# A state space mixer: the product by C on GpSimd, u B left in PSUM

## The chip, the cores and the metric

The program runs on one core of a Trainium2 chip. The time is device microseconds of one execution: 15,565.36 us, median of 3 runs (15,554.7 to 15,567.39). The core has five engines with a queue each, in which instructions start in order: TensorE (PE; matrix products, which land in PSUM), VectorE (DVE), ScalarE (ACT), GpSimd (POOL) and SyncE (SP, which issues transfers). The rows of weight loads, which TensorE overlaps with products, are PEld. SBUF is the large on-chip memory. PSUM has eight banks of 512 float32 columns on each of 128 partitions.

## The reference, cut to what matters

64 images of 121 tokens with 128 channels go through four pairs of layers, each added to its input: a mixer, and then a feed-forward layer (experts, two recurrent ones, a spectral one). All is float32. The change lies in the mixer, which runs four times:

```python
xz = x @ in_proj_w.T
xc, z = jnp.split(xz, 2, axis=-1)
xc = silu(conv(xc, conv_w) + conv_b)              # three taps
t = xc.transpose(0, 2, 1)
xs = jnp.stack([t, t], axis=1)                    # K = 2 directions
x_dbl = jnp.einsum('bkdl,kcd->bkcl', xs, x_proj_w)
dts, Bs, Cs = ...                                 # 8, 16 and 16 rows
delta = softplus(einsum('bkrl,kdr->bkdl', dts, dt_proj_w) + dt_proj_b)
A = -jnp.exp(A_logs)
dA = jnp.exp(delta[..., None] * A[None, :, :, None, :])
dBu = delta[..., None] * Bs * xs[..., None]
_, h = associative_scan(combine, (dA, dBu), axis=3)   # h[l] = dA[l] h[l-1] + dBu[l]
y = jnp.einsum('bkdln,bknl->bkdl', h, Cs) + Ds * xs
y = y[:, 0] + jnp.flip(y[:, 1], axis=-1)
out = layer_norm(y) * gelu(z) @ out_proj_w.T
```

The 121 tokens are the channels d of the recurrence, and it runs along l, the 256 inner channels. There are 16 states n.

## The kernel before

The activations X stay in SBUF during the whole program, tokens on the partitions. A mixer (`conv_layer`, L90) goes through the images in chunks of eight (c0, L121); eight chunks in each of four mixers make 32. A chunk begins with its layer norm, transposes, the convolution into t and the gate into g (L123 to L145; the one GpSimd instruction of a chunk, the memset of L126, zeroes the borders of xnT). Then come the scans, in two groups of four images (g0) and two directions (k): four blocks a chunk, 128 in all. At the end, in four rounds of two images, stand the layer norm over tokens, the gate, the output projection and the addition to X (L217 to L241).

A block begins with its preparation (L155 to L184). TensorE makes pb (the rows of B and C) and pd (the input of delta), each in two halves of 512 columns. S takes pb as three bf16 addends in 96 rows, made by casts of ScalarE (L164, L170, L171) and subtractions of VectorE (L165, L172). ScalarE and VectorE turn pd into delta = softplus(pd + b), by Abs and Relu (L168, L169), Exp (L175), two VectorE steps (L176, L177), Ln (L178) and two more steps (L179, L182), and u = delta t (L184). All are tiles of 121 partitions by 1024 columns, four images of 256.

The inner loop (L195) then runs over the 16 states, 2048 times in the whole program:

- L200: TensorE spreads row n of B over the partitions into pB, and row n of C into pC, by a selecting matrix sel; two matrix products of 512 columns each.
- L203: ScalarE writes exp(A delta) into one of three tiles dA, whose first column of each image stays zero.
- L208: VectorE writes u pB into hs; L209 scans hs in place, with dA; L212 multiplies hs by pC in place.
- L213 calls `add_to_y`, whose L192 adds hs to the sum py, by a matrix product with the identity, in two halves of 512 columns. For the second direction it reads hs backwards. A float32 product of 512 columns shows as two rows in the profile, so a state has four rows of L192.

The buffers: hs has three; S, u and delta have two. PSUM's eight banks are split between the pool ps_bc (two buffers of two banks, tag "bc": one goes to pB and one to pC), ps_y (py, two banks) and ps (two buffers of one bank, tag "mm", for all else: pb, pd, the convolution, the transposes, the rounds at the end).

The Tile framework puts each engine's instructions into an order when the program is built, and sets semaphores for the dependencies of tiles. Instructions that stand apart in the source, such as the preparation of a block and the states of the one before, can so stand mixed in an engine's queue. In the program before, TensorE's queue in the loop reads: py of state n-1, pC of n, pB of n+1, py of n, and so on.

Of the kernel before, what the change touches and what calls it, by code (L numbers as in the profile page):

```python
# [8 lines left out]
F32 = mybir.dt.float32  # L9
BF16 = mybir.dt.bfloat16  # L10
AF = mybir.ActivationFunctionType
ALU = mybir.AluOpType
AX = mybir.AxisListType
PSUM = bass.MemoryType.PSUM
DRAM = bass.MemoryType.DRAM

D = 121  # tokens of an image: the SSM's channels
C = 128  # model channels
L = 256  # inner channels: the SSM's sequence
NS = 16  # SSM states  # L20
E = 64  # experts
NF = 35  # STU filters: 16 phi, 16 alternating phi, 3 taps of the autoregression
FG = 7  # filters at a time
BANDS = ((0, 15), (15, 30), (30, 60), (60, 121))  # tokens that 4, 3, 2, 1 scales reach


class Ctx:
    """What all parts of the program share."""
# [12 lines left out]
def bcast(ap, n):  # L41
    """[P, G] -> [P, G, n]"""
    return ap.unsqueeze(2).to_broadcast([ap.shape[0], ap.shape[1], n])


def layer_norm(cx, pool, dst, src, eps):
    """Over the channels of each token: dst, src are [D, G, C]."""
    nc = cx.nc
    G = src.shape[1]
    mean = pool.tile([D, G], F32, name="ln_mean")  # L50
    nc.vector.reduce_sum(mean, src, axis=AX.X)
    nc.vector.tensor_scalar_mul(mean, mean, 1.0 / C)
    nc.vector.tensor_sub(dst, src, bcast(mean, C))
    sq = pool.tile([D, G, C], F32, name="ln_sq", bufs=1)
    nc.scalar.activation(sq, dst, AF.Square)
    rstd = pool.tile([D, G], F32, name="ln_rstd")
    nc.vector.reduce_sum(rstd, sq, axis=AX.X)
    nc.scalar.activation(rstd, rstd, AF.Sqrt, bias=eps[:D], scale=1.0 / C)
    nc.vector.reciprocal(rstd, rstd)
    nc.vector.tensor_mul(dst, dst, bcast(rstd, C))  # L60


def conv_weights(cx, l, wp):
    """Starts the loads of a mixer's weights."""
    nc, a, w = cx.nc, cx.a, {}

    def load(name, shape, src):
        w[name] = wp.tile(shape, F32, name=name)
        nc.sync.dma_start(w[name], src)

    p = f"L{l}_conv_"
    load("in_x", [128, 2, C], a[p + "in_x"].rearrange("(q p) c -> p q c", p=128))
    load("conv_wT", [128, 3, 2, L], a[p + "conv_wT"].rearrange("j (q p) o -> p j q o", p=128))
    load("in_zT", [C, L], a[p + "in_zT"])
    load("conv_b", [1, L], a[p + "conv_b"])
    load("x_dt", [8, 2, D], a[p + "x_dt"])
    load("dt_wT", [8, 2, D], a[p + "dt_wT"])
    load("dt_b", [D, 2], a[p + "dt_b"])
    load("A", [D, 2 * NS], a[p + "A_logs"])
    load("Ds", [D, 2], a[p + "Ds"])  # L80
    load("norm", [D, 2], a[p + "norm"])
    load("out_wT", [128, 2, C], a[p + "out_wT"].rearrange("(q p) c -> p q c", p=128))
    # B's and C's projections, three times over: for the three addends of their split.
    w["x_bc"] = wp.tile([D, 2, 3, 2 * NS], F32, name="x_bc")
    for i in range(3):
        nc.sync.dma_start(w["x_bc"][:, :, i, :], a[p + "x_bc"])
    return w


def conv_layer(cx, wts, pools, dA, sel, mean_w, ones_row):  # L90
    """x + SSM mixer(LN(x)). dA: tiles whose first column of each image is zero, which starts
    an image's recurrence afresh in a scan that runs over several images."""
    nc, X, NB = cx.nc, cx.X, cx.NB
    fixed, work, ps_bc, ps_y, ps = pools
    ident = cx.ident
    CB = min(8, NB)  # images of a chunk
    GB = 4  # images of a scan
    in_x, conv_wT, in_zT, conv_b, out_wT = (wts[x] for x in ("in_x", "conv_wT", "in_zT", "conv_b", "out_wT"))
    x_dt, dt_wT, dt_b, x_bc, A, Ds, norm = (wts[x] for x in ("x_dt", "dt_wT", "dt_b", "x_bc", "A", "Ds", "norm"))

    # in_proj and the convolution are both linear, with no bias between them: one [C, L] weight per tap.
# [6 lines left out]
    # So are dt's two projections.  # L108
# [12 lines left out]
    for c0 in range(0, NB, CB):  # L121
# [10 lines left out]
        t = work.tile([D, CB, L], F32, name="t")  # L132
# [15 lines left out]
        ysb = work.tile([D, CB, L], F32, name="ysb")  # L148
        for g0 in range(0, CB, GB):
            tg = t[:, g0 : g0 + GB, :].rearrange("p b l -> p (b l)")  # L150
            py = ps_y.tile([D, GB, L], F32, name="py")
            for k in range(2):
                # B and C of 512 columns at a time: a float32 is the sum of three bf16, exactly,
                # which one matmul by ones adds up again on all the partitions.
                S = work.tile([96, GB * L], BF16, name="S")  # L155
                rest = work.tile([96, GB * L], F32, name="rest", bufs=1)
                relu = work.tile([D, GB * L], F32, name="sp_relu", bufs=1)
                e = work.tile([D, GB * L], F32, name="sp_e", bufs=1)
                w = work.tile([D, GB * L], F32, name="sp_w", bufs=1)
# [13 lines left out]
                # softplus(v) = max(v, 0) + log1p(e), e = exp(-|v|);  # L173
                # log1p(e) = ln(w) - ((w - 1) - e) with w = fl(1 + e).
# [8 lines left out]
                u = work.tile([D, GB * L], F32, name="u")  # L183
                nc.vector.tensor_mul(u, df, tg)  # L184

                def add_to_y(src, w, start, stop):
                    """The second scan's share is flipped along the sequence."""
                    for h in range(0, GB, 2):
                        rhs = src[:, h : h + 2, :]
                        if k == 1:  # L190
                            rhs = rhs[:, :, ::-1]
                        nc.tensor.matmul(py[:, h : h + 2, :], w, rhs, start=start, stop=stop)  # L192

                add_to_y(t[:, g0 : g0 + GB, :], diag[:, k, :], k == 0, False)
                for n in range(NS):  # L195
                    pB = ps_bc.tile([D, GB * L], F32, name="pB", tag="bc")
                    pC = ps_bc.tile([D, GB * L], F32, name="pC", tag="bc")
                    for dst, row in ((pB, n), (pC, NS + n)):
                        for h in range(0, GB * L, 512):
                            nc.tensor.matmul(dst[:, h : h + 512], sel[:, row, :], S[:, h : h + 512], start=True, stop=True)  # L200
                    dAn = dA[turn % len(dA)]
                    turn += 1
                    nc.scalar.activation(  # L203
                        dAn[:, :, 1:], delta[:, :, 1:], AF.Exp, scale=A[:, k * NS + n : k * NS + n + 1]
                    )
                    hs = work.tile([D, GB, L], F32, name="hs", bufs=3)
                    hf = hs.rearrange("p b l -> p (b l)")
                    nc.vector.tensor_mul(hf, u, pB)  # L208
                    nc.vector.tensor_tensor_scan(  # L209
                        hf, dAn.rearrange("p b l -> p (b l)"), hf, 0.0, ALU.mult, ALU.add  # L210
                    )
                    nc.vector.tensor_mul(hf, hf, pC)  # L212
                    add_to_y(hs, ident[:D, :D], False, k == 1 and n == NS - 1)  # L213
            nc.scalar.copy(ysb[:, g0 : g0 + GB, :], py)

# [28 lines left out]
def conv_part(cx, l, wts):  # L244
    tc, nc = cx.tc, cx.nc
    with ExitStack() as ctx:
        enter = ctx.enter_context
        fixed = enter(tc.tile_pool(name=f"cf{l}", bufs=1))
        work = enter(tc.tile_pool(name=f"ck{l}", bufs=2))
        ps_bc = enter(tc.tile_pool(name=f"cpb{l}", bufs=2, space=PSUM))  # L250
        ps_y = enter(tc.tile_pool(name=f"cpy{l}", bufs=1, space=PSUM))
        ps = enter(tc.tile_pool(name=f"cp{l}", bufs=2, space=PSUM))
        # sel[:, r, :] picks row r of B, C: it has ones in rows r, 32 + r, 64 + r.
# [15 lines left out]
def moe_layer(cx, l):  # L269
    """x + experts(LN(x)): an expert takes a weighted sum of its 8 likeliest tokens and gives its  # L270
    result back to them, by the same weights. P has those weights, and zeros for other tokens."""
# [3 lines left out]
    EG = 4  # experts of a load  # L275
# [105 lines left out]
def rnn_layer(cx, l):  # L381
    """x + RNN over the tokens of BN(LN(x) W^T): channels on partitions, tokens by images beside."""
# [3 lines left out]
    with ExitStack() as ctx:  # L386
# [31 lines left out]
        # wx * s + (beta - mean * s), s = gamma / sqrt(var + eps)  # L418
# [8 lines left out]
        TS = 512 // NB if NB > 8 else 8  # steps of a PSUM bank  # L427
# [24 lines left out]
def stu_layer(cx, l):  # L452
    """x + the STU of LN(x) at four scales, by their weights. A scale sees, and gives, a prefix of
    the tokens, and the convolutions are causal: all scales share them, and a token's output matrices
    are the weighted sums of those of the scales that reach it."""
# [4 lines left out]
    with ExitStack() as ctx:  # L460
# [6 lines left out]
        # filters[s, f, t]: what token s gives to token t  # L467
# [3 lines left out]
        # Row s is phi, after D - 1 zeros, from place D - 1 - s on. The rows of a load step forward  # L471
        # in memory, so they come by descending s, and a matmul turns them round.
# [13 lines left out]
        # (-1)^(t - s)  # L486
# [8 lines left out]
        # the scales' weights: y_hard - y_soft + y_soft, on all partitions  # L495
# [15 lines left out]
        # the first of equal maxima alone: seen = 1 once one was  # L511
# [10 lines left out]
        # M[:, z]: band z's matrices, of scales 0 .. 3 - z  # L522
# [57 lines left out]
def metaformer_kernel(ctx: ExitStack, tc: tile.TileContext, a: dict, out: bass.AP):  # L580
    nc = tc.nc
# [3 lines left out]
    # The activations stay on the chip: tokens on partitions, images by channels beside.  # L585
# [19 lines left out]
def laid_out(inputs):  # L605
    """The inputs as the program reads them: slices, transposes and zero padding alone."""
# [55 lines left out]
```

## Time and profile before

| | |
|---|---|
| median of 3 runs | 15,565.36 us |
| span of the profiled execution | 15,534.4 us |
| mean granted clock of TensorE | 0.812 |
| L209, scan on VectorE | 2048 x 2289 ns |
| L208 and L212, products on VectorE | 2048 x 1212 and 1217 ns |
| L203, exponential on ScalarE | 2048 x 1145 ns |
| L192, sum into py on TensorE | 5444.3 us busy |
| L200, pB and pC on TensorE | 1373.8 and 1383.7 us busy |

The profile's span runs from the first to the last instruction of one execution. In the lines of groups the fields are: line, engine, operation, output from inputs, shapes, count | busy time in us, mean ns of one | idle time in us of the engine just before these instructions, and what ended most of it. In lines of the timeline they are: start and duration in us, engine, line, operation, count, and in brackets the idle time before with what ended it. In a line of stretches, the fields after the length are the busy times (with counts) of PE, PEld, VectorE, ScalarE and GpSimd, the granted clock as a share of full speed, and two fields on transfers.

The page shows the span in 40 equal slices, each digit the busy share of a slice in tenths:

```profile
PE   6777776766777777776777777777677777777799
...
DVE  8888888884888888887688888888488888888522
ACT  3333333322333333332333333323333333333222
POOL 0000000000000000000000000000000000000000
PEclk8888788876788888887788888888688888888899
```

The four mixers are the long stretches with VectorE at 8; the dips at slices 10, 19 and 20, and 29 and the last three slices are the feed-forward layers. A chunk takes 425 us.

### The profile page before, as it was taken

Reading aid. Unit: us, or ns where it says so; the run is one execution under the profiler, and the core shown is the slowest. Engines: PE = TensorE matmul, PEld = TensorE weight load, DVE = VectorE, ACT = ScalarE, POOL = GpSimd, SP = SyncE. Lnnn points to the kernel's source line nnn. Section 1 sums busy time; section 2 is a strip of 40 time slices with the busy share of each in tenths; the row PEclk is TensorE's granted clock in tenths of the full one; section 3 lists DMA queues with packets and bytes.
Section 4 is the critical chain, followed back from the end, with each engine's and each line's share of the span. In section 5 each row is a group of like instructions: output and inputs, shape, how many; then the busy total and the mean of one; then the engine's idle time right before and its main releaser. Section 6 shows DMA issues by size and latency. Waiting matters only on the chain.

```text
span 15534.4 us, 76849 instructions
## 1 busy us (share of the span) xinstructions
PE 11231.5 (72%) x28744; PEld 5111.1 (33%) x28744; DVE 11896.6 (77%) x9160; ACT 4972.8 (32%) x5572; POOL 4.3 (0%) x38
## 2 busy tenths in 40 slices
PE   6777776766777777776777777777677777777799
PEld 2322332225233323333332322322323232322466
DVE  8888888884888888887688888888488888888522
ACT  3333333322333333332333333323333333333222
POOL 0000000000000000000000000000000000000000
PEclk8888788876788888887788888888688888888899
DMA  0000000002000000000000000000000000000100
GB/s 16 0 0 0 0 0 0 1 18 84 0 0 0 0 0 0 0 1 1 3 0 0 0 0 0 0 0 1 1 0 0 0 0 0 0 0 0 28 4 6
DMA packets 84526, 66.42 MB, mean 4 GB/s; under 512 B 10547, under 2 KB 70839, under 8 KB 84151
## 3 DMA queue, kind: packets, MB, share of 16 engines
q1 hardware_dynamic: 82871, 59.41, 1.3%
q8 instruction: 225, 3.69, 0.1%
q10 hardware_dynamic: 1280, 2.10, 0.0%
q14 instruction: 150, 1.23, 0.0%
HBM read 55.43 MB, written 6.06 MB: 4 GB/s over the span
## 4 chain that ended last, share of the span: by engine, by line
DVE 53%; PE 37%; ACT 5%; issue 4%; SPq 0%; DVEq 0%; DMA 0%; ACTq 0%
DVE hs L209 20%; PE py L192 16%; DVE hs L212 14%; DVE hs L208 11%; PE acc L558 3%; PE pu L548 3%; PE pc L138 3%; PE pC L200 2%; DVE ystd L228 1%; PE pc L139 1%; PE pst L440 1%; PE po L239 1%; PE pb L163 1%; DVE sp_w L179 1%; DVE S L172 1%
## 5 line engine op out<-in xcount | busy, mean ns | idle before, releaser
L192 PE MATMUL py<-hs,ident 121*121 121x512 f32 x8192 | 5444.3, 800 | 2349.9 <-DVE hs L212 2343.1
L209 DVE TENSOR_TENSOR_SCAN hs<-dA,hs 121x1024 f32<-121x1024 f32 x2048 | 4687.9, 2289 | 136.1 <-DVE hs L208 5.5
L203 ACT ACTIVATE dA<-delta,A 121x1020 f32<-121x1020 f32 x2048 | 2338.3, 1145 | 6374.4 <-DVE hs L209 6372.4
L192 PEld LDWEIGHTS py<-hs,ident 121*121 121x121 f32 x8192 | 1711.6, 230 | 4884.1 <-DVE hs L212 3379.0
L212 DVE TENSOR_TENSOR hs<-hs,pC 121x1024 f32<-121x1024 f32 x2048 | 2492.2, 1217 | 428.6 <-PE pC L200 338.0
L208 DVE TENSOR_TENSOR hs<-u,pB 121x1024 f32<-121x1024 f32 x2048 | 2482.9, 1212 | 73.0 <-PE pB L200 69.2
L200 PEld LDWEIGHTS <-sel 96*121 96x121 bf16 x8192 | 1271.8, 155 | 2852.4 <-issue 2584.3
L200 PE MATMUL pC<-S,sel 96*121 96x512 bf16 x4096 | 1383.7, 421 | 498.5 <-DVE hs L208 498.5
L200 PE MATMUL pB<-S,sel 96*121 96x512 bf16 x4096 | 1373.8, 420 | 261.5 <-DVE hs L208 189.7
L165 DVE TENSOR_TENSOR rest<-pb,S 96x512 f32<-96x512 f32 x256 | 173.5, 678 | 701.7 <-ACT S L164 701.7
L552 DVE COPY U<-pu 128x363 f32<-128x363 f32 x320 | 171.3, 536 | 652.0 <-PE pu L548 651.4
L228 DVE RECIPROCAL ystd<-ystd 121x512 f32<-121x512 f32 x128 | 427.5, 3340 | 199.0 <-ACT ystd L227 199.0
L548 PE MATMUL pu<-filt,u 121*128 121x484 f32 (+1 forms) x1280 | 469.5, 524 | 11.5 <-DVE U L552 7.5
L558 PE MATMUL acc<-U,M 128*128 128x120 f32 (+2 forms) x2240 | 477.6, 372 | 0.4
L138 PE MATMUL pc<-w_conv,xnT 128*121 128x256 f32 x1536 | 430.2, 419 | 2.2 <-ACT xnT L131 2.2
L163 PE MATMUL pb<-t,x_bc 121*96 121x512 f32 x512 | 342.1, 756 | 120.5 <-DVE rest L165 74.3
L234 PE MATMUL pyt<-ident,ysb 121*128 121x121 f32 x512 | 115.8, 369 | 414.2 <-DVE ysb L231 414.0
L554 ACT COPY U<-pu 128x484 f32<-128x484 f32 x320 | 180.5, 564 | 677.9 <-PE pu L548 675.8
L558 PEld LDWEIGHTS acc<-U,M 128*128 128x128 f32 x2240 | 334.8, 190 | 135.7 <-issue 115.0
L167 PE MATMUL pd<-t,w_dt 121*121 121x512 f32 x512 | 296.1, 662 | 44.6 <-DVE rest L165 44.6
L138 PEld LDWEIGHTS pc<-w_conv,xnT 128*121 128x121 f32 x1536 | 280.4, 196 | 126.9 <-issue 77.0
L225 PE MATMUL pv<-ysq,mean_w 121*121 121x512 f32 x256 | 195.4, 857 | 173.9 <-ACT ysq L223 173.9
(176 smaller groups left out, 7475.3 us busy)
## 6 DMA issues: line engine op xcount, KB each, us to landing
w1g<-in_L_ffn_weight_dram SPq DMA_DIRECT2D x16, 1024.0 KB
w2g<-in_L_ffn_weight_dram SPq DMA_DIRECT2D x64, 256.0 KB
X<-in_x_dram SPq DMA_DIRECT2D x8, 484.0 KB
out_dram<-X SPq DMA_DIRECT2D x8, 484.0 KB
conv_wT<-in_L_conv_conv_wT_dram SPq DMA_DIRECT2D x4, 768.0 KB
O<-og ACTq DMA_DIRECT2D x16, 128.0 KB
oe<-O SPq DMA_DIRECT2D x4, 512.0 KB
ahead<-in_L_ffn_phi_dram SPq DMA_DIRECT2D x1, 915.1 KB
```

Of the source, the lines that this page charges most:

```text
L138: nc.tensor.matmul(pc[:, i, :], xnT[:, b + i, j : j + D], w_conv[:, j, :], start=(j == 0), stop=False)
L163: nc.tensor.matmul(pb, x_bc[:, k].rearrange("p i n -> p (i n)"), tg[:, cols], start=True, stop=True)
L167: nc.tensor.matmul(pd, w_dt[:, k, :], tg[:, cols], start=True, stop=True)
L192: nc.tensor.matmul(py[:, h : h + 2, :], w, rhs, start=start, stop=stop)
L200: nc.tensor.matmul(dst[:, h : h + 512], sel[:, row, :], S[:, h : h + 512], start=True, stop=True)
L203: nc.scalar.activation(dAn[:, :, 1:], delta[:, :, 1:], AF.Exp, scale=A[:, k * NS + n : k * NS + n + 1])
L208: nc.vector.tensor_mul(hf, u, pB)
L209: nc.vector.tensor_tensor_scan(hf, dAn.rearrange("p b l -> p (b l)"), hf, 0.0, ALU.mult, ALU.add)
L212: nc.vector.tensor_mul(hf, hf, pC)
L228: nc.vector.reciprocal(std, std)
L548: nc.tensor.matmul(pu[:, : fb - fa, :], u[:, b, :], filt[:, f0 + fa : f0 + fb, :], start=True, stop=True)
L558: nc.tensor.matmul(acc[z], M[:, z, f0 + f, :], U[:, f, :, t0:t1], start=(f0 + f == 0), stop=(f0 + f == NF - 1),)
```

## The change

In the inner loop four things change. pB keeps both buffers of the tag "bc". pC becomes two tiles of 512 columns from the pool ps (tag "mm"), and ScalarE copies each into a new SBUF tile Cs, of which there are two buffers. L208's product is written back to pB in place of hs, and the scan reads it there and writes hs. The product by C reads Cs instead of pC and is issued on GpSimd. The names of the lines after are L202 and L205 (pB, pC), L206 (the copies), L209 (the exponential), L214 (the product u B), L215 (the scan) and L218 (the product by C); lines behind the loop move down by six. The sums into py stay as they are.

```diff
                 for n in range(NS):
                     pB = ps_bc.tile([D, GB * L], F32, name="pB", tag="bc")
-                    pC = ps_bc.tile([D, GB * L], F32, name="pC", tag="bc")
-                    for dst, row in ((pB, n), (pC, NS + n)):
-                        for h in range(0, GB * L, 512):
-                            nc.tensor.matmul(dst[:, h : h + 512], sel[:, row, :], S[:, h : h + 512], start=True, stop=True)
+                    Cs = work.tile([D, GB * L], F32, name="Cs")
+                    for h in range(0, GB * L, 512):
+                        nc.tensor.matmul(pB[:, h : h + 512], sel[:, n, :], S[:, h : h + 512], start=True, stop=True)
+                    for h in range(0, GB * L, 512):
+                        pC = ps.tile([D, 512], F32, name="pC", tag="mm")
+                        nc.tensor.matmul(pC, sel[:, NS + n, :], S[:, h : h + 512], start=True, stop=True)
+                        nc.scalar.copy(Cs[:, h : h + 512], pC)
                     dAn = dA[turn % len(dA)]
                     turn += 1
                     nc.scalar.activation(
                         dAn[:, :, 1:], delta[:, :, 1:], AF.Exp, scale=A[:, k * NS + n : k * NS + n + 1]
                     )
                     hs = work.tile([D, GB, L], F32, name="hs", bufs=3)
                     hf = hs.rearrange("p b l -> p (b l)")
-                    nc.vector.tensor_mul(hf, u, pB)
+                    nc.vector.tensor_mul(pB, u, pB)
                     nc.vector.tensor_tensor_scan(
-                        hf, dAn.rearrange("p b l -> p (b l)"), hf, 0.0, ALU.mult, ALU.add
+                        hf, dAn.rearrange("p b l -> p (b l)"), pB, 0.0, ALU.mult, ALU.add
                     )
-                    nc.vector.tensor_mul(hf, hf, pC)
+                    nc.gpsimd.tensor_mul(hf, hf, Cs)
                     add_to_y(hs, ident[:D, :D], False, k == 1 and n == NS - 1)
```

## The prediction

> **What bounds the kernel now.** I read the page's busy shares, then the costliest groups, then one stretch of the timeline inside a mixer, then who waits for whom.
>
> ```profile
> PE 11231.5 (72%) x28744; PEld 5111.1 (33%) x28744; DVE 11896.6 (77%) x9160; ACT 4972.8 (32%) x5572; POOL 4.3 (0%) x38
> ...
> L209 DVE TENSOR_TENSOR_SCAN hs<-dA,hs 121x1024 f32<-121x1024 f32 x2048 | 4687.9, 2289 | 136.1 <-DVE hs L208 5.5
> ...
> L212 DVE TENSOR_TENSOR hs<-hs,pC 121x1024 f32<-121x1024 f32 x2048 | 2492.2, 1217 | 428.6 <-PE pC L200 338.0
> L208 DVE TENSOR_TENSOR hs<-u,pB 121x1024 f32<-121x1024 f32 x2048 | 2482.9, 1212 | 73.0 <-PE pB L200 69.2
> ```
>
> VectorE does 9,663 us of its 11,897 in these three groups, 4.72 us for each of the 2048 states. Idle time before them is small (637.7 us in all): inside the loop VectorE is the bound, and nothing makes it wait for long. ScalarE is a third busy, GpSimd idle. So the change takes a quarter off the bound; what decides is whether VectorE can stay fed afterwards.
>
> ```profile
> 2260.28 3.64 PE L192 MATMUL py<-hs,ident 121*121 121x512 f32 x4 [0.72 <-DVE hs L212]
> ...
> 2264.19 0.59 PE L200 MATMUL pB<-S,sel 96*121 96x512 bf16 x2
> 2264.39 1.22 DVE L212 TENSOR_TENSOR hs<-hs,pC 121x1024 f32<-121x1024 f32 x1 [0.64 <-PE pC L200]
> 2265.53 1.21 DVE L208 TENSOR_TENSOR hs<-u,pB 121x1024 f32<-121x1024 f32 x1
> 2265.66 1.98 PE L192 MATMUL py<-hs,ident 121*121 121x512 f32 x4 [0.88 <-DVE hs L212]
> 2266.84 2.29 DVE L209 TENSOR_TENSOR_SCAN hs<-dA,hs 121x1024 f32<-121x1024 f32 x1
> 2267.48 0.60 PE L200 MATMUL pC<-S,sel 96*121 96x512 bf16 x2
> 2267.92 0.59 PE L200 MATMUL pB<-S,sel 96*121 96x512 bf16 x2
> ```
>
> The sum into py waits for a finished product (0.05 us after L212 ends), then come the next pC and pB, all under the following L208 and L209: 3.2 us of TensorE work beside 3.5 us of VectorE. The same four py rows take 1.98 us or 3.64 us; the granted clock, 0.81 on average, alternates between full and half, so 38% of the time is at half.
>
> I count by chunk (eight images). GpSimd's 32 memsets of L126 mark chunks, 425.3 us apart (482.50, 907.78, 1332.46).
>
> ```profile
> 2185.75:2611.06 425.31, 302.90 (x713) 127.63 (x712) 352.81 (x252) 140.56 (x147) 0.12 (x1) 0.82 0.00 0
> ```
>
> That is VectorE busy for 352.8 us of 425.3 (third pair of numbers). A chunk holds 4 blocks (two groups, two directions) of 16 states.
>
> **Removed.** 64 products a chunk of 1.217 us leave VectorE: -77.9 us.
>
> **Products in place, in PSUM.** L208 now writes pB, and the scan reads pB. No row of VectorE writes PSUM. A PSUM input costs nothing visible (L212 with pC 1217 ns, L182 from SBUF alone 1210 ns). I take zero; bounded by those 7 ns either way for both instructions, +-30 us in the program.
>
> **Copies of C.** 4096 copies of 121x512 on ScalarE; the row of that kind is L554, 128x484 from PSUM in 0.564 us, so 0.59 us each, 2,420 us. ScalarE goes from 4,973 to 7,390 us, covered by VectorE in the loop: a state costs ScalarE 1.15 + 1.18 us against 3.51 us on VectorE. Where that cover is missing, they count below.
>
> **The product on GpSimd.** Its rows:
>
> ```profile
> L126 POOL MEMSET xnT<- 128x16 f32 x32 | 3.7, 116 | 13720.1 <-PE pz L144 10389.9 <-PE px L447 2113.8 <-PE px L376 1216.4
> masks.py:199 POOL TENSOR_SCALAR_AFFINE_SELECT ident<-ident 128x128 f32<-128x128 f32 x1 | 0.3, 292 | 0.0
> masks.py:197 POOL MEMSET ident<- 128x128 f32 x1 | 0.2, 204 | 0.3 <-POOLq L652 0.3
> ```
>
> Lower bound: the memsets' slope, (204-116)/112 = 0.79 ns a column, 0.9 us for 1024 columns with its start, but it reads nothing. Upper: the select reads one operand, 292 ns for 128 columns, 2.34 us for 1024; with a second operand at the same price 4.67. I take 2.34: the select is nearest in kind, its start would not repeat eight times, and the second operand costs something. The Trainium skill ("GPSIMD Engine Reference", section Performance versus the Vector engine) has a measured 4497 ns for a float32 add of two operands at 2048 columns; half, an estimate of 2.25 us, would take 60 us off my sum.
>
> **What the product's new place makes late.** In the built program's queues the loop runs in groups of three states a, b, c. VectorE: product a, product b, scan a, scan b, product c, scan c, then product d. TensorE: ... py a, py b, first half of pB d, **py c, second half of pB d**, pC d. pB has both "bc" buffers now, yet product d still stands behind py c, py c behind GpSimd's product c, and that behind scan c, VectorE's last work. So VectorE stops once in three states for: GpSimd 2.34 + py 1.98 + half a pB 0.30 + three handovers of 0.05 = 4.77 us at full clock; 2.34 + 3.64 + 0.53 + 0.15 = 6.66 us at half. With 38% at half that is 5.5; the idle TensorE may lose some clock, so 5.6. VectorE's own work for three states is 3 x 3.51 = 10.5 us, so a group takes 16.1 us, 5.4 a state, against 4.7 to 5 now. A block has five groups and one more state, so five such stops; 20 a chunk: 112 us, where today's loop idles 637.7/32 = 19.9. **+92 us.**
>
> **Between blocks.** L165 to L184 now stand in one run on VectorE, with no state between, so their handovers are bare. The second L165 waits for pb and the cast S (1.10 + 0.58 + handovers: 1.9); L172 for two casts of 1.04 (2.2); L176 for L168, L169, L175 (0.69 + 0.68 + 1.05, less 1.22 of L172: 1.3); L179 for Ln, queued on ScalarE behind four copies of C (4 x 0.59 + a table load 1.28 + 1.06, less L176 and L177: 3.3). Sum 8.7 a block. Today: L172, L179 and L176 idle 103.1 + 66.0 + 36.8 us over 128 blocks, 1.6 a block, and L165 some 0.6 outside the chunk starts (701.7 us, of which about 19.6 at each of 32 starts, unchanged by the edit). 4 x (8.7 - 2.2) = **+26 us.**
>
> **The chunk's end.** The four rounds L221 to L241 likewise stand in a row; today some lie between states. Each waits for Sqrt (longest today 3.5 us) and for po (longest 3.9): 4 x 7.4 = 29.6, where L228 and L241 idle (199.0 + 248.1)/32 = 14.0 today. **+16 us.**
>
> **Sum.** -77.9 + 92 + 26 + 16 = +56 us a chunk, times 32 = +1,790 us on the span of 15,534.4: 17,325. The median of the runs lies 31 us above that span, so **17,350 us**. What the program does outside the mixers isn't touched.
>
> **A rule on the shared port.** No row of before has VectorE and GpSimd side by side. The Trainium skill ("SBUF — State Buffer", section Who interferes with whom) says that a VectorE instruction with two SBUF inputs excludes a GpSimd one that reads SBUF, and that one with a single SBUF input doesn't. By it the loop is free, since product and scan each take one input from pB, and only the runs between blocks could collide. No run here shows it yet.
>
> **Rivals.**
> 1. *GpSimd becomes the bound.* From about 2.9 us a product, the three products no longer fit beside scan b, product c and scan c (5.8 us). A group is then 4.72 us (products a, b and scan a) + three GpSimd products + 3.2 us (py, half a pB, handovers): 18.4 at 3.5 us, hence +2.3 x 640 stops = +1,470: 18,820; at 4.67 us 21,100. For it: the second operand. Against: the select's start counted eight times. 10%.
> 2. *VectorE and GpSimd exclude each other in the loop.* Then three products add to VectorE's work: 10.5 + 7.0 + 3.2 = 20.7 us a group, +4.6 x 640 = +2,940: 20,300 us. Nothing in the trace speaks for or against. 6%.
> 3. *Faster: the saving is kept.* If the queue doesn't hold product d back, -77.9 x 32 leaves 13,070 us. With the losses outside the loop it pays from a stop under (77.9 + 19.9 - 26 - 16)/20 = 2.8 us. But py and pB alone are 2.43 at full clock, which leaves 0.37 for GpSimd, below its lower bound of 0.9. 3%; near zero change 2%.
> 4. *ScalarE becomes the bound.* 2.33 us a state against 5.4: the copies would have to cost 4.2 us instead of 1.18. Counted with the likeliest.
>
> **How the numbers follow.** The likeliest, 79%, runs from a product of 0.9 us (-1.4 x 640 = -920: 16,430) to the stops all at half clock (+1.06 x 640 = +680: 18,030). The range leaves out the lowest end and takes in part of rival 1: 16,750 to 18,500. Faster by over 0.2% (what a measurement can tell from no change) 3%, within 2%, slower 95%.
>
> **What would show it.** Right: L214 and L215 keep 1.21 and 2.29 us; some 3,580 us (112 x 32) of VectorE idle before L214, ended by TensorE's pB; py waits for GpSimd; VectorE's busy time down by 2,490 us. Wrong: L218 far from 2.3 us, L214 or L215 longer beside GpSimd, no stop every third state, or idle between blocks near today's.

## The result, and the profile after

17,303.5 us median (17,298.9 to 17,304.56, 4 runs), against 15,565.96 us for the kernel before: a ratio of 1.1116 (95% interval 1.1101 to 1.1132). The prediction said 17,350 us, 16,750 to 18,500. The profiled execution's span is 17,297.0 us, the mean granted clock 0.755.

The page after: busy shares, the chain of work that ended last by engine (it is followed back from the last instruction; "issue" is time in which an engine waited for nothing that the profile shows), and the costliest groups (fields as in the part before):

```profile
PE 11733.1 (68%) x28744; PEld 5269.0 (30%) x28744; DVE 9518.4 (55%) x7112; ACT 6964.6 (40%) x9540; POOL 4795.1 (28%) x2086
...
PE 46%; DVE 22%; issue 13%; POOL 10%; ACT 8%; SPq 0%; DMA 0%; POOLq 0%; DVEq 0%; ACTq 0%
...
L218 POOL TENSOR_TENSOR hs<-hs,Cs 121x1024 f32<-121x1024 f32 x2048 | 4790.7, 2352 | 8203.6 <-DVE hs L215 8192.5
L192 PE MATMUL py<-hs,ident 121*121 121x512 f32 x8192 | 5398.7, 812 | 1237.8 <-POOL hs L218 1219.8
L215 DVE TENSOR_TENSOR_SCAN hs<-dA,pB 121x1024 f32<-121x1024 f32 x2048 | 4608.1, 2276 | 103.1 <-ACT Cs L206 2.5
L214 DVE TENSOR_TENSOR pB<-u,pB 121x1024 f32<-121x1024 f32 x2048 | 2439.5, 1220 | 3313.6 <-PE pB L202 3299.9
L206 ACT COPY Cs<-pC 121x512 f32<-121x512 f32 x4096 | 2201.4, 588 | 4082.8 <-PE pC L205 3206.9
```

No engine is busier than 68%. VectorE lost 2,378 us of work and gained 3,241 us of idle time ahead of one instruction, the product u B, in which it waits for TensorE's pB. Of the chain that ended last, 53% lay on VectorE before and 22% does now; 46% lies on TensorE and 10% on GpSimd.

One group of three states, in the timeline after (columns: start and duration in us, engine, line, operation, count, in brackets the idle time before and what ended it):

```profile
2329.30 2.36 DVE L214 TENSOR_TENSOR pB<-u,pB 121x1024 f32<-121x1024 f32 x2 [5.62 <-PE pB L202]
...
2331.57 4.46 DVE L215 TENSOR_TENSOR_SCAN hs<-dA,pB 121x1024 f32<-121x1024 f32 x2
...
2334.00 4.66 POOL L218 TENSOR_TENSOR hs<-hs,Cs 121x1024 f32<-121x1024 f32 x2 [7.82 <-DVE hs L215]
2335.95 1.21 DVE L214 TENSOR_TENSOR pB<-u,pB 121x1024 f32<-121x1024 f32 x1
...
2336.40 5.49 PE L192 MATMUL py<-hs,ident 121*121 121x512 f32 x8 [1.38 <-POOL hs L218]
2337.29 2.29 DVE L215 TENSOR_TENSOR_SCAN hs<-dA,pB 121x1024 f32<-121x1024 f32 x1
...
2339.72 2.35 POOL L218 TENSOR_TENSOR hs<-hs,Cs 121x1024 f32<-121x1024 f32 x1 [1.05 <-DVE hs L215]
2341.73 0.38 PE L202 MATMUL pB<-S,sel 96*121 96x512 bf16 x1
2342.12 1.98 PE L192 MATMUL py<-hs,ident 121*121 121x512 f32 x4
2343.94 0.38 PE L202 MATMUL pB<-S,sel 96*121 96x512 bf16 x1
2344.16 0.59 PE L205 MATMUL pC<-S,sel 96*121 96x512 bf16 x2
2344.36 2.36 DVE L214 TENSOR_TENSOR pB<-u,pB 121x1024 f32<-121x1024 f32 x2 [4.78 <-PE pB L202]
```

Read it from the end. Product d (2344.36) waits for the second half of its pB (2343.94), which stands behind py c (2342.12). Py c starts 0.05 us after GpSimd's product c (2339.72 + 2.35), and that began when scan c ended. So VectorE stands still for 4.78 us, and a group takes 15.06 us for 10.3 us of work. There are 640 such waits, as many as groups counted (20 a chunk), and each of them ends 0.04 us after a half of pB that ran behind py c. They are of two kinds. In 321 of them py c starts within 0.1 us of the end of GpSimd's product c, as here; py a and py b take 5.2 to 6.0 us there, and the wait is 4.83 us on average. In the other 319 py a and py b take 6.0 to 6.8 us, py c starts later, behind them, and the wait is 5.49 us.

The span splits into VectorE's work and its idle time before three sets of instructions: the products and scans of the loop; L165, L172, L176 and L179 (preparation); and the first subtraction, the reciprocal and the last addition of the rounds at a chunk's end. The sums are made from the rows of VectorE's groups in each profile. Two of the larger ones outside the loop, before:

```profile
L165 DVE TENSOR_TENSOR rest<-pb,S 96x512 f32<-96x512 f32 x256 | 173.5, 678 | 701.7 <-ACT S L164 701.7
...
L228 DVE RECIPROCAL ystd<-ystd 121x512 f32<-121x512 f32 x128 | 427.5, 3340 | 199.0 <-ACT ystd L227 199.0
```

and after:

```profile
L234 DVE RECIPROCAL ystd<-ystd 121x512 f32<-121x512 f32 x128 | 429.1, 3353 | 582.5 <-ACT ystd L233 582.5
...
L165 DVE TENSOR_TENSOR rest<-pb,S 96x512 f32<-96x512 f32 x256 | 173.4, 677 | 825.7 <-ACT S L164 825.7
```

All of them together:

| span, us | work | idle in loop | in preparation | at chunk's end | all else |
|---|---|---|---|---|---|
| before 15,534.4 | 11,896.6 | 637.7 | 907.6 | 666.1 | 1,426.4 |
| after 17,297.0 | 9,518.4 | 3,416.7 | 1,718.7 | 1,196.8 | 1,446.4 |
| difference +1,762.6 | -2,378.2 | +2,779.0 | +811.1 | +530.7 | +20.0 |

### The profile page after: what moved, and what is told of

It is laid out like the page before. It is cut to its first block, busy times and chain, and to the rows that moved or that the text cites. A ratio compares the mean times of both kernels' runs of the same rounds, so it can differ in the third digit from the quotient of the medians.

```text
span 17297.0 us, 84375 instructions
## 1 busy us (share of the span) xinstructions
PE 11733.1 (68%) x28744; PEld 5269.0 (30%) x28744; DVE 9518.4 (55%) x7112; ACT 6964.6 (40%) x9540; POOL 4795.1 (28%) x2086
## 4 chain that ended last, share of the span: by engine, by line
PE 46%; DVE 22%; issue 13%; POOL 10%; ACT 8%; SPq 0%; DMA 0%; POOLq 0%; DVEq 0%; ACTq 0%
PE py L192 25%; DVE hs L215 11%; POOL hs L218 10%; DVE pB L214 3%; PE acc L564 3%; PE pu L554 3%; DVE ystd L234 2%; PE pc L138 2%; ACT Cs L206 2%; PE pB L202 2%; PE po L245 2%; PE pv L231 1%; PE pc L139 1%; DVE sp_w L179 1%; DVE u L184 1%
## 5 line engine op out<-in xcount | busy, mean ns | idle before, releaser
L218 POOL TENSOR_TENSOR hs<-hs,Cs 121x1024 f32<-121x1024 f32 x2048 | 4790.7, 2352 | 8203.6 <-DVE hs L215 8192.5
L215 DVE TENSOR_TENSOR_SCAN hs<-dA,pB 121x1024 f32<-121x1024 f32 x2048 | 4608.1, 2276 | 103.1 <-ACT Cs L206 2.5
L214 DVE TENSOR_TENSOR pB<-u,pB 121x1024 f32<-121x1024 f32 x2048 | 2439.5, 1220 | 3313.6 <-PE pB L202 3299.9
L206 ACT COPY Cs<-pC 121x512 f32<-121x512 f32 x4096 | 2201.4, 588 | 4082.8 <-PE pC L205 3206.9
L192 PEld LDWEIGHTS py<-hs,ident 121*121 121x121 f32 x8192 | 1986.4, 257 | 4380.4 <-POOL hs L218 2369.1
L209 ACT ACTIVATE dA<-delta,A 121x1020 f32<-121x1020 f32 x2048 | 2324.0, 1146 | 2126.1 <-DVE hs L215 2012.0
L202 PE MATMUL pB<-S,sel 96*121 96x512 bf16 x4096 | 1541.7, 442 | 2209.3 <-DVE hs L215 2006.2
L205 PE MATMUL pC<-S,sel 96*121 96x512 bf16 x4096 | 1470.8, 392 | 462.0 <-ACT Cs L206 280.5
L202 PEld LDWEIGHTS <-sel 96*121 96x121 bf16 x4096 | 541.2, 148 | 3289.3 <-DVE hs L215 2558.6
L205 PEld LDWEIGHTS <-sel 96*121 96x121 bf16 x4096 | 562.8, 137 | 1100.7 <-issue 971.3
L165 DVE TENSOR_TENSOR rest<-pb,S 96x512 f32<-96x512 f32 x256 | 173.4, 677 | 825.7 <-ACT S L164 825.7
L163 PE MATMUL pb<-t,x_bc 121*96 121x512 f32 x512 | 280.9, 630 | 201.9 <-DVE rest L165 152.5
L242 ACT COPY yT<-pyt 128x484 f32<-128x484 f32 x128 | 71.9, 562 | 846.0 <-PE pyt L240 846.0
```

The source lines that it names most:

```text
L202: nc.tensor.matmul(pB[:, h : h + 512], sel[:, n, :], S[:, h : h + 512], start=True, stop=True)
L205: nc.tensor.matmul(pC, sel[:, NS + n, :], S[:, h : h + 512], start=True, stop=True)
L206: nc.scalar.copy(Cs[:, h : h + 512], pC)
L209: nc.scalar.activation(dAn[:, :, 1:], delta[:, :, 1:], AF.Exp, scale=A[:, k * NS + n : k * NS + n + 1])
L214: nc.vector.tensor_mul(pB, u, pB)
L215: nc.vector.tensor_tensor_scan(hf, dAn.rearrange("p b l -> p (b l)"), pB, 0.0, ALU.mult, ALU.add)
```

## The experiments

Theory 1 is the prediction's: the order of TensorE's queue makes the stop, since pB of state d stands behind the py that waits for GpSimd. Its main rivals: GpSimd's rate sets the pace wherever py stands (theory 2); VectorE and GpSimd exclude each other (theory 3). The kernel before, run beside these, took 15,543.8 to 15,568.4 us in single runs. All ratios are to the kernel before, run beside each experiment.

### The sums into py one and two states late

In the source only the place at which py of a state is issued moves, and with two states hs gets a fourth buffer. The edit with two states (with one it says `> 1`, and hs keeps three buffers):

```diff
+                late = []
                 for n in range(NS):
...
-                    hs = work.tile([D, GB, L], F32, name="hs", bufs=3)
+                    hs = work.tile([D, GB, L], F32, name="hs", bufs=4)
...
                     nc.gpsimd.tensor_mul(hf, hf, Cs)
-                    add_to_y(hs, ident[:D, :D], False, k == 1 and n == NS - 1)
+                    late.append(hs)
+                    if len(late) > 2:
+                        add_to_y(late.pop(0), ident[:D, :D], False, False)
+                while late:
+                    src = late.pop(0)
+                    add_to_y(src, ident[:D, :D], False, k == 1 and not late)
```

> Only the place of the sums into py changes: the source issues py of a state one state later, so that TensorE's queue gets the next pB ahead of the last group's py more often. Theory 1 (the stop is a matter of TensorE's queue: product d waits for its pB, which stands behind py c and so behind GpSimd's product c): the idle time before L214, 3,300 us after the change, falls to about a third, and the time to 15,300 us (15,000 to 15,900). Theory 2 (GpSimd's product, at 2.35 us twice a VectorE one, paces the loop wherever py stands): the time stays within 2% of 17,300 us.

> As the kernel before it, but py two states late, with a fourth buffer for hs. TensorE's queue then has pB and pC of the next states ahead of the py that waits for GpSimd, one by one. Theory 1: idle before L214 under 300 us, time about 14,600 us (14,300 to 15,000), below the kernel before the change; what is left against 13,070 us is the idle between blocks and at the chunk's end. GpSimd's product keeps its 2.35 us. Theory 2: no less than 16,800 us.

One state late: 15,740.3 us, ratio 1.0117 (1.0102 to 1.0132), within theory 1's range; VectorE's loop idle is 1,547 us, 1,407.5 of it before the product u B, 42% of what it was and not the third expected. Two states late: **14,708.2 us**, ratio 0.9457 (0.9443 to 0.9471), as theory 1 had it. The groups with two states late:

```profile
L219 POOL TENSOR_TENSOR hs<-hs,Cs 121x1024 f32<-121x1024 f32 x2048 | 4815.7, 2354 | 5602.3 <-DVE hs L216 5302.6
L216 DVE TENSOR_TENSOR_SCAN hs<-dA,pB 121x1024 f32<-121x1024 f32 x2048 | 4668.5, 2285 | 242.4 <-ACT dA L210 5.9
...
L215 DVE TENSOR_TENSOR pB<-u,pB 121x1024 f32<-121x1024 f32 x2048 | 2467.8, 1211 | 154.2 <-PE pB L203 140.8
```

GpSimd's product takes as long as before, 2.35 us, and ScalarE makes the same copies, but the wait for pB has gone from 3,299.9 to 140.8 us, and with it 2,595 us of time. So theory 2 is out, and with it ScalarE as the bound. The framework also put VectorE's instructions into another order here (product and scan by turns, where they stood in groups of three states), and the fourth buffer wasn't tried without the later sums. So these runs alone don't show that the stop is a matter of TensorE's queue; the timeline after does, where product d waits for a pB that stands behind py c in each of the 640 stops. The same change of engine is 11% slower or 5% faster, by where the sum into py is issued.

### u B in SBUF instead of PSUM

```diff
-                    nc.vector.tensor_mul(pB, u, pB)
+                    nc.vector.tensor_mul(hf, u, pB)
                     nc.vector.tensor_tensor_scan(
-                        hf, dAn.rearrange("p b l -> p (b l)"), pB, 0.0, ALU.mult, ALU.add
+                        hf, dAn.rearrange("p b l -> p (b l)"), hf, 0.0, ALU.mult, ALU.add
                     )
```

> The change without its PSUM part: u B goes to hs in SBUF and the scan reads hs, the product by C stays on GpSimd and reads Cs. pB is free once the product u B is done, not only after the scan, and TensorE's queue has the next pB ahead of py of the last state. The scan now has two SBUF inputs. Theory 1 with no exclusion between VectorE and GpSimd: most of the stop is gone by the earlier pB, about 15,300 us (15,000 to 15,700), L215 stays at 2.28 us and L218 at 2.35 us. Theory 3 (a VectorE instruction with two SBUF inputs and a GpSimd one exclude each other, as the skill's page on SBUF has it): rows of L215 or L218 grow by up to the other's length, VectorE or GpSimd stands still about 2.3 us a state, and the time is 17,500 us or more.

> The sums two states late, with u B in hs in SBUF instead of pB, so that the scan has two SBUF inputs beside GpSimd's product and TensorE's queue holds nothing up. If VectorE and GpSimd exclude each other at such instructions: L215's kind 2.8 us and GpSimd's product 3.3 us or more, as in the run with u B in SBUF, 16,000 us (15,500 to 17,000), 1,000 us or more above 14,708 us. If they don't, and the long rows of that run were only waits: 14,400 to 14,800 us.

On top of the change: 17,643.6 us, ratio 1.1344 (1.1327 to 1.1361). With the sums two states late: 16,557.9 us, ratio 1.0642 (1.0626 to 1.0658), so 1,850 us more than the same kernel with u B in PSUM. Both came out on the side of exclusion. The groups of the second of them:

```profile
L219 POOL TENSOR_TENSOR hs<-hs,Cs 121x1024 f32<-121x1024 f32 x2048 | 6804.1, 3341 | 5484.5 <-DVE hs L216 5465.9
...
L216 DVE TENSOR_TENSOR_SCAN hs<-dA,hs 121x1024 f32<-121x1024 f32 x2048 | 6062.1, 2970 | 161.5 <-ACT dA L210 3.7
...
L215 DVE TENSOR_TENSOR hs<-u,pB 121x1024 f32<-121x1024 f32 x2048 | 2452.0, 1208 | 419.8 <-PE pB L203 399.6
```

and two rows of its timeline:

```profile
2369.72 6.50 POOL L219 TENSOR_TENSOR hs<-hs,Cs 121x1024 f32<-121x1024 f32 x2 [22.33 <-DVE hs L216]
...
2373.92 4.45 DVE L216 TENSOR_TENSOR_SCAN hs<-dA,hs 121x1024 f32<-121x1024 f32 x1
```

The scan with two SBUF inputs takes 2.97 us on average instead of 2.285, and GpSimd's product grows from 2.354 to 3.341 us. The two rows shown say how. Of the two products, which take 6.50 us together, the first began beside a scan that ended at 2371.76 and took 4.19 us; the second took 2.35 and ended at 2376.22. The scan that began at 2373.92, beside the second of them, ends 2.15 us after that product, at 2378.37: it spent the first 2.3 of its 4.45 us waiting. The 128 scans of this run with no product beside them keep 2.28 us. The product u B, with pB from PSUM and one SBUF input, keeps its 1.21 us beside the same GpSimd work. The waiting lies inside the rows, where it reads as slow work. In the changed kernel, with one SBUF input in each, scan and product run side by side at their own lengths (2.276 and 2.352 us). So theory 3 holds for the variant and not for the change, and in single rows the one that started first keeps its length. It agrees with what the Trainium skill ("SBUF — State Buffer", section Who interferes with whom) says of VectorE instructions with two SBUF inputs.

### GpSimd's share of the stop

```diff
-                    nc.gpsimd.tensor_mul(hf, hf, Cs)
+                    nc.gpsimd.tensor_mul(hf[:, :512], hf[:, :512], Cs[:, :512])
```

> GpSimd multiplies only the first 512 of the 1024 columns by C; the other half goes into py without the factor C, so this leaves out part of the computation. TensorE's queue keeps its groups of three with py c ahead of the second half of pB d. It sizes GpSimd's share of the stop. Theory 1: a product of about 1.2 us instead of 2.35, each of 640 stops shorter by 1.15 us, so -740 us: 16,550 us (16,350 to 16,750). Theory 4 (the stop is set by TensorE at half clock or by ScalarE's copies of C, and GpSimd's length hides beside them): less than 200 us gained.

16,881.1 us, ratio 1.0854 (1.0836 to 1.0872): 422 us less than after the change, between the two expectations. Its rows of GpSimd's product and of the wait:

```profile
L218 POOL TENSOR_TENSOR hs<-hs,Cs 121x512 f32<-121x512 f32 x2048 | 2600.0, 1270 | 9990.2 <-DVE hs L215 9970.8
...
L214 DVE TENSOR_TENSOR pB<-u,pB 121x1024 f32<-121x1024 f32 x2048 | 2430.5, 1221 | 2755.7 <-PE pB L202 2742.3
```

The product is 1.08 us shorter, the 640 stops only 0.87 us (2742.3/640 = 4.28 against 5.16). Loop idle falls by 591 us, and 245 us come back in preparation (1,963.8 against 1,718.7). The first difference is that of the two kinds of stop. In the timeline after, where py a and py b run at half clock throughout (8 rows in 6.61 us instead of 5.49), py c waits for py b and not for GpSimd, and the wait is 5.62 instead of 4.78 us. With the half product py c starts over 0.1 us after GpSimd's product in 506 of the 640 stops, where it was 319; in these stops GpSimd's length no longer counts in full. The second difference stays open: with a shorter product the framework also built another order of VectorE's instructions, which this run can't tell apart.

### One part at a time

> The kernel before, with one part of the change alone: u B is written back to pB and the scan reads it there; the product by C stays on VectorE and reads pC. Theory 1: writing and reading PSUM costs VectorE nothing, L208 1.21 us, L209 2.28 us; pB is held 2.3 us longer, but the product by C on VectorE (1.2 us) covers the next pB (0.6 us at full clock, 1.06 at half); 15,400 to 15,850 us. Rival: PSUM as output or as the scan's input is slower on VectorE, 0.1 us or more in a state, or the longer hold stops VectorE: over 15,900 us.

u B in PSUM alone, on the kernel before: 15,871.8 us, ratio 1.0201 (1.0184 to 1.0218), just over the range of theory 1 and under the rival's. Its groups of VectorE in the loop:

```profile
L209 DVE TENSOR_TENSOR_SCAN hs<-dA,pB 121x1024 f32<-121x1024 f32 x2048 | 4679.9, 2285 | 160.4 <-DVE pB L208 6.4
...
L212 DVE TENSOR_TENSOR hs<-hs,pC 121x1024 f32<-121x1024 f32 x2048 | 2493.5, 1218 | 615.6 <-PE pC L200 517.7
L208 DVE TENSOR_TENSOR pB<-u,pB 121x1024 f32<-121x1024 f32 x2048 | 2503.1, 1222 | 111.2 <-PE pB L200 106.2
```

L208 took 1,222 and L209 2,285 ns, where it was 1,212 and 2,289: PSUM itself costs at most 10 ns a state. Loop idle rose from 637.7 to 887.2 us; pB, with one buffer here, is now held until the scan's end. Preparation (953.1 us) and the chunk's end (645.3) idle about as in the kernel before (907.6 and 666.1).

> The whole change but the engine: the product by C stays on VectorE and reads Cs. Theory 1 (a part of the loss has nothing to do with GpSimd: pC's copies on ScalarE and pC's place among the banks of pb and pd put the preparation of a block and the rounds at a chunk's end behind the loop; 26 + 16 us a chunk in the prediction's sum): VectorE's idle before L165, L172, L176, L179, L234 and L247 is like that after the change, idle before L214 under 300 us, and the time is 16,500 us (16,200 to 16,900). Rival (those waits came from GpSimd being late with a block's last states): the idle there is that of the kernel before, 15,450 to 15,900 us.

All of the change but the engine: 16,090.5 us, ratio 1.0343 (1.0328 to 1.0358), below the expected 16,200 to 16,900. VectorE's waits for others in this run (us in all, times, longest):

```profile
DVE rest L165 <- ACT S L164: 1003.8, 160, 26.2
...
DVE X L247 <- PE po L245: 499.6, 128, 3.9
DVE ystd L234 <- ACT ystd L233: 477.7, 128, 7.9
DVE sp_w L179 <- ACT sp_w L178: 414.9, 128, 4.3
DVE S L172 <- ACT S L171: 377.9, 128, 3.0
```

Preparation idles 1,836.4 and the chunk's end 1,093.7 us, close to the change (1,718.7 and 1,196.8): nearly all of this part of the loss is there without GpSimd. What I missed is the gain beside it: the loop's idle fell from 637.7 to 13.7 us, and work by 200 us. VectorE's instructions stand in pairs of two states here, and rows that don't depend on each other overlap by some 0.1 us.

> The kernel before, with ScalarE's two copies of C to SBUF added (4096 of 0.59 us) and the product by C on VectorE reading Cs; pC stays one tile of 1024 columns in the tag bc, u B in hs. It separates two causes of the idle between blocks that the run without GpSimd left together. Theory A (pC's place among the buffers of pb and pd: the next block's pb gets a bank only after the last state's pC, so its preparation can't start among the states): here the tag mm is free in the loop again, VectorE's idle before L165, L172, L176, L179 and in the rounds stays near that of the kernel before (908 and 666 us), and the time is 15,300 to 15,800 us. Theory B (the copies in ScalarE's queue delay the casts, Ln and Sqrt): the idle is like that without GpSimd (1,836 and 1,094 us), 16,000 us or more.

```diff
+                    Cs = work.tile([D, GB * L], F32, name="Cs")
+                    for h in range(0, GB * L, 512):
+                        nc.scalar.copy(Cs[:, h : h + 512], pC[:, h : h + 512])
...
-                    nc.vector.tensor_mul(hf, hf, pC)
+                    nc.vector.tensor_mul(hf, hf, Cs)
```

14,910.2 us, ratio 0.9584 (0.9568 to 0.96), faster than either theory had it. Its groups of VectorE and of the copy:

```profile
L212 DVE TENSOR_TENSOR_SCAN hs<-dA,hs 121x1024 f32<-121x1024 f32 x2048 | 4657.4, 2279 | 9.1 <-ACT dA L206 6.9
L203 ACT COPY Cs<-pC 121x512 f32<-121x512 f32 x4096 | 2195.0, 588 | 2489.4 <-DVE hs L215 1671.2
...
L215 DVE TENSOR_TENSOR hs<-hs,Cs 121x1024 f32<-121x1024 f32 x2048 | 2475.9, 1214 | 1.0
L211 DVE TENSOR_TENSOR hs<-u,pB 121x1024 f32<-121x1024 f32 x2048 | 2442.4, 1198 | 35.2 <-PE pB L200 22.0
```

Preparation idles 844.2 us, no more than in the kernel before, with all 4096 copies in ScalarE's queue: so the copies don't move preparation behind the loop. Nor does u B in PSUM, by the run with it alone (953.1 us). What is left is theory A, pC's place among the buffers of pb and pd, and with it pB's second buffer; no run moved these alone. The chunk's end, at 920.3, lies between the two; A explains only a part of it. The loop idles 45.3 us, 592 less than before, and VectorE's work fell by 231 us. Neither theory had this gain. ScalarE's copy frees pC's buffer earlier, and the framework also built another order of VectorE's instructions; which of the two brought it is not shown.

### Preparation of the next block among the states

On the kernel with the sums two states late, L155 to L184 become a function, called for the first block ahead of the loop and for each next one behind state 11:

```diff
+        ready = prepare(*blocks[0])
         for g0 in range(0, CB, GB):
...
+                S, delta, u = ready
...
+                    if n == 11:
+                        at = blocks.index((g0, k)) + 1
+                        ready = prepare(*blocks[at]) if at < len(blocks) else None
```

> The sums two states late, and the preparation of the next block (L155 to L184) issued in the source behind state 11 of the block before it, within a chunk. Theory 1 (what is left over 13,070 us is mostly VectorE's idle between blocks): L165, L172, L176 and L179 lose their idle but at the chunk's start, some 1,300 us, and preparation overlaps states: 13,450 us (13,200 to 13,900). Rival (preparation's two-input instructions collide with GpSimd's products, or ScalarE's queue with its table loads holds the exponentials up): 14,200 us or more.

**13,932.6 us**, ratio 0.8955 (0.8942 to 0.8968), the fastest of all here, a little over its range. Idle in preparation fell from 2,115.0 to 1,012.6 us. Two of its instructions with two SBUF inputs now stand beside GpSimd's product in three of a chunk's four blocks, and a third never does:

```profile
L173 DVE SCALAR_TENSOR_TENSOR sp_e<-sp_w,sp_e 121x1024 f32<-121x1024 f32 x128 | 351.7, 2748 | 4.1
L168 DVE TENSOR_TENSOR S<-rest,S 32x1024 bf16<-32x1024 f32 x128 | 319.9, 2499 | 98.1 <-ACT S L167 95.1
...
L175 DVE TENSOR_TENSOR sp_w<-sp_w,sp_e 121x1024 f32<-121x1024 f32 x128 | 155.4, 1214 | 62.2 <-ACT sp_w L174 62.2
```

With the preparation behind the loop, the first two took 1,226 and 1,217 ns. Here the 32 of each in a chunk's first block, with no product beside them, keep 1,225 and 1,217 ns, and the 96 others take 3,255 and 2,926. That is 359 us; VectorE's work as a whole grew by 287, a quarter of the 1,102 us of idle time won: the rival's collision is there. The last two instructions of a preparation, delta and u, have two SBUF inputs as well and keep 1,200 ns; GpSimd's product that starts beside them is the one that grows, to 3.2 us, and its mean is 2,471 ns instead of 2,354.

## Why the prediction was right

By its own terms, per chunk (differences of the table above over 32):

| step | predicted, us | measured, us |
|---|---|---|
| products removed from VectorE | -77.9 | -74.3 |
| stops in the loop | +92 | +86.8 |
| between blocks | +26 | +25.3 |
| chunk's end | +16 | +16.6 |
| all else | 0 | +0.6 |
| sum | +56 | +55.1 |

- **The price of GpSimd's product**, the least known: 2.34 us from the select's row, 2.352 measured; the estimate of 2.25 us beside it was 4% low. That the two errors in the 2.34 cancel (a start counted eight times, one operand missing) was luck.
- **The stop** is in the timeline as forecast, and the experiments that moved py agree: right in mechanism and in count (640), and close in size, 5.6 us predicted and 5.16 measured. The full-clock sum of 4.77 us is the wait shown, 4.78. The addition for half clock was right by luck. I priced py c itself at 3.64 us in 38% of the stops, and the mean clock did fall, to 0.755. But py c took 1.88 to 1.98 us, full clock, in all 640 stops. What made half of them longer is that py a and py b ran longer at half clock before it (6.0 to 6.8 us against 5.2 to 6.0), so that py c started late behind py b: a wait of 5.49 us on average against 4.83.
- **Between blocks** the sum was right, its terms less so: the waits of L165, L172, L176 and L179 were priced at 1.9, 2.2, 1.3 and 3.3 us a block and measured 1.8, 3.3, 1.0 and 2.7.
- **At the chunk's end** two errors cancel. The waits for Sqrt and for po, priced at 29.6 us a chunk, took 33.8: in the first of the four rounds, 32 times in all, the wait for Sqrt is 8.5 to 9.1 us instead of 3.5, and its input pv (L231) comes right behind a py in TensorE's queue. The wait for pm (L221, now L227), which the sum left out, fell by 3.3 us a chunk.
- **The cause of both**: the run without GpSimd shows that nearly all of it belongs to the rest of the change. The prediction took it from the built queues without naming a cause. The runs with the copies and with u B in PSUM alone leave pC's and pB's buffers for preparation; a part of the chunk's end comes with the copies, and the rest is open.
- **The removed products** brought 3.6 us a chunk less than their rows say. Neighbouring rows of VectorE overlap by up to a tenth of a microsecond, and the busy time counts this once. Summed over the trace the overlap fell from 378 to 265 us, but not among the loop's own rows (196 before, 221 after): it fell among the others, most of which no longer stand between states.
- **Writing and reading PSUM** was taken as free, and is, to 10 ns.
- **The median** was put 31 us above the profiled span; it lay 6.5 us above it.
- **The rivals.** GpSimd was the bound neither here nor with the stop gone. Exclusion in the loop did not happen, and the variant shows that it would have without the PSUM part. The first rival's limit of 2.9 us holds for two products beside 5.8 us (those of a and b), not for the three that it names. The third rival's condition, a queue that doesn't hold product d back, is what the two kernels with the sums two states late establish: it was a property of one order and not of the edit.

## What to carry to other kernels

Work taken off the bound engine is only won if its next input isn't queued behind the result of the moved work: look in the built queue of the engine that feeds it for what stands ahead of that input, and issue the consumer of the slower result a state or two later. Beside GpSimd, give VectorE's instructions with two inputs one of them from PSUM, or expect rows of both engines to grow. Where a new tile joins a ring of buffers, ask which early work used to find a free buffer there.

## What the runs showed of the hardware beyond that

GpSimd's float32 product took 2,352 ns for 1024 columns and 1,270 for 512: by a straight line through the two, 2.11 ns a column and 0.19 us of start. A copy of C on ScalarE that costs 2,195 us of that engine's time made the kernel before 4.2% faster by itself, though VectorE, the bound engine, has as many instructions as before.
